# Head 6 aggregated in the block scheme, and the second layer's attention vector products spread over heads 0 to 5

## The chip, the cores and the metric

The kernel runs on one core of a Trainium2 chip. The metric is the device time of one execution in microseconds. TensorE (PE) multiplies matrices, VectorE (DVE) and ScalarE (ACT) do elementwise work, GpSimd (POOL) and SyncE (SP) here mostly issue transfers (DMAs). "PEld" in the profile is TensorE's loading of weights, which overlaps its matmuls.

## The reference, cut to what matters

Two graph attention layers, a residual and a layer norm, for N = 512 nodes and D = 768 features. Layer 1 has H = 8 heads, layer 2 has one.

```python
def gat_layer(x, W, a_s, a_d, b, edge_index, concat):
    h = (x @ W).reshape(n, H, C)
    alpha_s = jnp.einsum('nhc,hc->nh', h, a_s)
    alpha_d = jnp.einsum('nhc,hc->nh', h, a_d)
    e = jax.nn.leaky_relu(alpha_s[src] + alpha_d[dst], NEG_SLOPE)
    # softmax of e over the edges that enter a node -> alpha
    msg = h[src] * alpha[:, :, None]
    out = jax.ops.segment_sum(msg, dst, num_segments=n)
    return out.reshape(n, H * C) + b
h = jax.nn.elu(gat_layer(x, W1, a_src1, a_dst1, b1, ...))   # 512 x 6144
x = layernorm(x + gat_layer(h, W2, a_src2, a_dst2, b2, ...))
```

The kernel treats the graph as a dense 512 x 512 matrix of edge counts, so that a head's attention is a dense matrix P and its aggregation a product with P. The second layer's `h @ W2` is a sum over the heads of layer 1: (head's output, 512 x 768) times (that head's 768 rows of W2).

## The kernel before, in words

There is one instruction stream per engine, written out by hand (no scheduler moves anything); each engine takes its own in that order, and the order in the Python text is therefore the order on each engine. SP's and POOL's transfers too are issued in the order of the text, each once what it overwrites has been read.

First the edge counts are made and heads 0 and 1 are projected (up to L813). Then a loop over h from 0 to 6 (L816) does, for each step:

- **load_w1(h + 2)** (L818): SP loads W1 of the head after next into the tiles of slot "w2" (`w2t1`, `w20`, `w21`), POOL adds a part to them. In the last step the second layer's attention vectors, spread to all 128 rows, go into the tiles `w2t2` and `w2t4` instead, and W2 of head 7 into slot "w2" (L820 to L825).
- **Aggregation of head h**, the product of features and P. In steps 0 to 5 by `mixed` (L741): a block scheme, in which halves of the features times halves of P make seven block products instead of eight. Each of three column groups c runs seven products of two matmuls with 256 columns (L763). It needs sums of blocks, of the features in `gS` (`left_sums`, L717, four VectorE additions of 768 columns) and of P in `pS` (`right_sums`, L730, four of 512 columns). They are made a step earlier, during the projection, and stand between its matmuls. `fill` is a list of VectorE work that `mixed` puts between its own: the attention logits of the next head (`half_logits`, L312). In step 6 by `aggregate` (L705): six column groups c of four matmuls with 512 columns (L709), no sums. Between these VectorE does the next head's logits (c < 2) and then the twelve products of L841: W2 of head 7, row block by row block (k from 0 to 5), times the two attention vectors of layer 2, each summed along the row into `V`. `V` (768 x 2) serves at the end to get head 7's share of the second layer's logits from `gT` directly (L964).
- `elu` (L694) after either kind: ScalarE makes the parts, VectorE joins them into `gT` (L703).
- **load_a(h + 2)** (L845): SP loads the attention vectors `a_s` and `a_d` of the head after next.
- **second** (L347): `gT` times W2 of head h, in a block scheme with matmuls of 384 columns (all by the helper at L304), added up in `h2` and `u2`. Meanwhile VectorE and ScalarE make the attention matrix of head h + 1 (`lift` L448, `leak` L454, `rank` L457, `weigh` L663). In steps 0 to 5 it is transposed by DMA: ScalarE separates the bytes' halves (`turn_out`, L684), SP issues the transpose (L688), ScalarE joins the result into `PT` (`turn_in`, L690). In step 6 TensorE transposes (`turn`, L675) and ScalarE copies (L679). At the end of steps 0 to 5 SP loads W2 of head h + 1.
- **projection** of head h + 2 (steps 0 to 5, L900 to L922): 14 pairs n of a product (L304) and its emptying from PSUM. Right operands that are sums, t2 and t4, lie in `w2t2` and `w2t4`; VectorE makes them with L296 and L297 at n = 1 and 3. P6 (n = 4 and 5) reads t2, P4 (n = 8 and 9) reads t4. L339 empties P6. The sums for the next step's `mixed` stand at n = 1 to 8, but only where the next step uses `mixed`.

After the loop head 7 is aggregated plainly, multiplied by W2, and the second layer's attention, aggregation and layer norm follow.

Of the kernel before, what the change touches and what calls it, by code (L numbers as in the profile page):

```python
# [8 lines left out]
F32 = mybir.dt.float32  # L9
# [27 lines left out]
def gat_pass(  # L37
# [89 lines left out]
    def load_a(h, a_s, a_d):  # L127
        A[h] = []
        for name, a in (("a_s", a_s), ("a_d", a_d)):
            v = wpool.tile([P, D], F32, name=name)  # L130
            nc.sync.dma_start(v, row_bcast(a))
            A[h].append(v)
# [134 lines left out]
    xS = keep.tile([P, 3, HK, HN], F32, name="xS")  # L267
    scr = keep.tile([P, D], BF16, name="scr")
    V = keep.tile([P, DC, 2], F32, name="V")
    al2 = keep.tile([P, 2, NT], F32, name="al2")  # L270
    own2 = keep.tile([P, NT], F32, name="own2")

# [39 lines left out]
    def half_logits(h, t):  # L312
        return [lambda al=al, a=a, sign=sign: nc.vector.scalar_tensor_tensor(
            scr, HS[h][:, t, :], sign, a, op0=ALU.mult, op1=ALU.mult, accum_out=al[:, t:t + 1])
            for al, a, sign in zip(AL[h], A[h], (1.0, -1.0))]

    def logits(h, feats, t):
        for al, a, sign in zip(AL[h], A[h], (1.0, -1.0)):
            nc.vector.scalar_tensor_tensor(scr, feats[:, t, :], sign, a, op0=ALU.mult,
                                           op1=ALU.mult, accum_out=al[:, t:t + 1])  # L320
# [384 lines left out]
    def aggregate(h, c):  # L705

        ps = mm.tile([P, 512], F32, name="mm")
        for s in range(NT):
            nc.tensor.matmul(ps[:, :N], HS[h][:, s, c * P:(c + 1) * P], PT[:, s, :],  # L709
                             start=(s == 0), stop=(s == NT - 1))  # L710
        return elu(h, c, ps[:, :N], slice(0, N), "r")
# [29 lines left out]
    def mixed(h, A_, B_, fill):  # L741

        tt = nc.vector.tensor_tensor
        behind = []

        def some(n):
            for f in fill[:n]:
                f()
            del fill[:n]

        for c in range(HK):
            u = work.tile([P, HN], F32, name="u")
            w = work.tile([P, HN], F32, name="w")
            zr = work.tile([P, N], F32, name="zr", bufs=3)
            bank = {}

            def part(p, over=None):
                if over is None:
                    bank[p] = mm.tile([P, 512], F32, name="mm")
                else:  # L760
                    bank[p] = bank[over]
                for k in range(2):
                    nc.tensor.matmul(bank[p][:, :HN], A_[p][:, k, c * P:(c + 1) * P], B_[p][:, k, :],  # L763
                                     start=over is None and k == 0, stop=k == 1, skip_group_check=True)
                return bank[p][:, :HN]

            nc.scalar.copy(u, part("P1"))  # L767
            if behind:

                behind = behind[0]()  # L770
            tt(u, u, part("P6"), op=ALU.add)
            tt(w, u, part("P7"), op=ALU.add)
            for f in behind[:1]:
                f()
            near_l = elu(h, c, part("P2", over="P1"), near, "l")
            some(1)
            tt(zr[:, far_], part("P5"), w, op=ALU.subtract)
            for f in behind[1:]:
                f()
            tt(zr[:, near], u, part("P4", over="P7"), op=ALU.add)  # L780
            near_l()
            tt(u, part("P3", over="P5"), u, op=ALU.subtract)
            some(-(-len(fill) // (2 * (HK - c) - 1)))

            def others(c=c, u=u, zr=zr):
                return [elu(h, HK + c, zr, slice(0, N), "r", spare=zr), elu(h, c, u, far_, "l", spare=u)]
            behind = [others]
        return behind[0]()
# [24 lines left out]
    for f in rsums[2:]:  # L813
        f()
    besides = [lsums[3], *some_logits]
    for h in range(H - 1):  # L816
        if h + 2 < H:
            load_w1(h + 2)()  # L818
        else:
            A[H] = []  # L820
            for j, a in ((2, a_src2[0]), (4, a_dst2[0])):
                v = wpool.tile([P, HK, HALF], F32, name=f"w2t{j}").rearrange("p k n -> p (k n)")[:, :D]
                nc.sync.dma_start(v, row_bcast(a))
                A[H].append(v)
            last_sum = load_w2(H - 1, "w2")  # L825
        GA, gsums = left(gT, gS)
        if h + 2 < H:
            finish = mixed(h, AA, BB, besides + [p for t in ((0, 1) if h else (0, 1, 3)) for p in half_logits(h + 1, t)])
        else:
            finish = []  # L830
            for c in range(DC):
                finish.append(aggregate(h, c))
                if c:
                    finish.pop(0)()
                if c < 2:
                    logits(h + 1, HS[h + 1], c)
                else:

                    for k in ((0, 1), (2,), (3,), (4, 5))[c - 2]:
                        for v, a, sign in zip(range(2), A[H], (1.0, -1.0)):  # L840
                            nc.vector.scalar_tensor_tensor(scr, W2[H - 1][k // HK][:, k % HK, :], sign, a,  # L841
                                                           op0=ALU.mult, op1=ALU.mult, accum_out=V[:, k, v:v + 1])
        besides = []
        if h + 2 < H:
            load_a(h + 2, a_src1[h + 2], a_dst1[h + 2])  # L845
        pairs = second(h, GA, B2)
        for m, _ in pairs[:2]:
            m()
        pairs[0][1]()
        for f in finish:  # L850
            f()
        gsums[0]()
        pairs[1][1]()
        gsums[1]()
        if pending:
            pending.pop(0)()
        spread(h + 1)
        pairs[2][0]()
        gsums[2]()
        pairs[3][0]()  # L860
        gsums[3]()
        if pending:
            pending.pop(0)()
        pairs[2][1]()
        pairs[3][1]()
        last = h + 2 == H
        q = [lift(h + 1, 0)]
        for n in range(2, 7):
            (m0, e0), (m1, e1) = pairs[2 * n:2 * n + 2]
            m0()  # L870
            if not last:
                m1()
            if n < 6:
                leak(q[n - 2])
                rank(q[n - 2], n - 2)
            if n < 5:
                q.append(lift(h + 1, n - 1))
            if last:

                if n > 3:  # L880
                    turn(q[n - 4], n - 4)
                if n == 6:
                    weigh(q[3], 3)
                m1(lambda: turn(q[3], 3) if n == 6 else None)
            if not last and n == 6:
                turn_in(0)
                weigh(q[2], 2)
                turn_out(q[2], 2)
            e0()
            if last and 2 < n < 6:  # L890
                weigh(q[n - 3], n - 3)
            if not last and 3 < n < 6:
                weigh(q[n - 4], n - 4)
                turn_out(q[n - 4], n - 4)
            if not last and n == 6:
                weigh(q[3], 3)
                turn_out(q[3], 3)
                load_w2(h + 1)()
            e1()
        if h + 2 < H:  # L900
            B_, sums = right(W1[h + 2], "w2")
            pairs = projection(h + 2, XA, B_)
            for n in range(14):
                pairs[n][0]()
                if n == 0:
                    turn_in(1)
                    B2, sums2 = right(W2[h + 1], "w1")
                if n in (1, 3):
                    sums[n // 2]()
                if n == 1:  # L910
                    AA, sums3 = left_sums(h + 1) if h + 3 < H else (None, [])
                pairs[n][1]()
                if n in (2, 4):
                    turn_in(1 + n // 2)
                if n == 5 and h + 3 < H:
                    BB, sums3 = right_sums()
                if 1 <= n < 9 and h + 3 < H:
                    sums3.pop(0)()
                if n in (9, 10):
                    sums2.pop(0)()  # L920
                if n in (11, 13):
                    logits(h + 2, HS[h + 2], 2 + (n - 11) // 2)  # L922
        else:
            last_sum()
            B2, sums2 = right(W2[H - 1], "w1")
# [5 lines left out]
    nc.sync.dma_start(b2_bc, row_bcast(b2))  # L931
    AL[H] = (al2[:, 0, :], al2[:, 1, :])
    GA, gsums = left(gT, gS)
    finish = []
    parts = [(h2[:, 2 + i, L], i, ALU.add) for i in range(2)] + [
        (h2[:, j + i, R], i, ALU.subtract) for j in (2, 0) for i in range(2)]
# [140 lines left out]
```

## Time and profile before

| what | value |
|---|---|
| median of 3 runs (lowest, highest) | 653.67 us (653.57, 653.68) |
| the profiled execution, its span | 653.82 us, 651.8 us |
| TensorE busy | 640.2 us, 98% of the span |
| VectorE busy | 507.4 us, 78% |
| ScalarE busy | 273.8 us, 42% |
| GpSimd busy | 47.0 us, 7% |
| bytes moved by DMA, mean rate | 90.88 MB, 139 GB/s |

How to read it: "busy" sums an engine's instructions over the span; a busy engine need not be the one that sets the end. The chain of work that ended last is followed back from the last instruction to what released it, so it names what did set the end. A group's line gives the number of instructions after "x", then busy time and the mean duration of one in ns; TensorE's matmuls overlap, so that their durations add up to more than their busy time. For each matmul of the text in this data type the trace holds two records. In a timeline, brackets give the idle time ahead of an instruction and what ended it. Some stages by start time: `mixed` of steps 0 to 5 starts at 82.4, 156.5, 229.5, 302.5, 375.7 and 448.7 us, `aggregate` of step 6 at 521.7, of head 7 at 571.6; the final aggregation runs from 623.6 on.

### The profile page before, as it was taken

How to read it: one execution, taken by the hardware profiler on the slowest of the kernel's cores; microseconds unless marked ns; L12 is line 12 of the kernel's file. 1: busy time of each engine (PE TensorE's matmuls, PEld its weight loads, DVE VectorE, ACT ScalarE, POOL GpSimd, SP SyncE). 2: the span in 40 equal slices, each digit the busy share in tenths (PEclk: the TensorE clock that was granted, in tenths of full speed). 3: DMA queues.
4: the chain of work that ended last, by engine and by line, in shares of the span. 5: the costliest groups of instructions: out<-in, count | busy, mean ns of one | idle time of the engine just before them, and what ended most of it. 6: DMA issues, size and time to landing. Idle time of an engine off the chain costs nothing.

```text
span 651.8 us, 7058 instructions
## 1 busy us (share of the span) xinstructions
PE 640.2 (98%) x2347; PEld 397.6 (61%) x2347; DVE 507.4 (78%) x1102; ACT 273.8 (42%) x469; POOL 47.0 (7%) x90
## 2 busy tenths in 40 slices
PE   8999999999999999999999999999999999999995
PEld 4544586557755586557755586557755545645553
DVE  7989989968777777858777777858775588876775
ACT  5774744530736044531736044521736043243440
POOL 1310020011000010011000010011000000000000
PEclk9999999999999999999999999999999999999998
DMA  9993398196506790296406790296407865000122
GB/s 316 328 202 86 74 332 215 37 264 199 123 0 173 157 269 23 45 265 200 112 1 174 169 267 12 49 267 198 108 1 202 203 181 133 24 1 0 34 56 77
DMA packets 74186, 90.88 MB, mean 139 GB/s; under 512 B 36710, under 2 KB 58526, under 8 KB 74142
## 3 DMA queue, kind: packets, MB, share of 16 engines
q1 hardware_dynamic: 60478, 68.72, 33.6%
q0 software_dynamic: 12976, 20.65, 18.3%
q10 hardware_dynamic: 688, 0.98, 0.5%
q8 instruction: 20, 0.33, 0.2%
q14 instruction: 24, 0.20, 0.1%
HBM read 78.02 MB, written 1.57 MB: 122 GB/s over the span
## 4 chain that ended last, share of the span: by engine, by line
PE 97%; ACT 1%; DVE 1%; issue 0%; DVEq 0%
PE mm L304 64%; PE mm L763 17%; PE mm L709 6%; PE mm L1029 3%; PE held L304 2%; PE tr L542 1%; PE bc L177 1%; ACT os L514 1%; PE bc L445 0%; PE bc L542 0%; PE tr L957 0%; PE tr L678 0%; ACT xT L205 0%; PE mm L204 0%; DVE os L516 0%
## 5 line engine op out<-in xcount | busy, mean ns | idle before, releaser
L304 PE MATMUL mm<-w,gT 128*128 128x384 f32 x288 | 97.4, 487 | 0.0
L304 PE MATMUL mm<-w,xT 128*128 128x384 f32 x264 | 88.4, 488 | 0.0
L304 PEld LDWEIGHTS mm<-w,gT 128*128 128x128 f32 x288 | 53.9, 190 | 35.7 <-issue 2.0
L304 PEld LDWEIGHTS mm<-w,xT 128*128 128x128 f32 x264 | 49.8, 190 | 35.7 <-ACT os L514 0.8
L462 ACT ACTIVATE q<-q,nmax 128x512 f32<-128x512 f32 x36 | 25.8, 721 | 89.8 <-DVE nmax L460 89.8
L304 PE MATMUL mm<-w1t,gS 128*128 128x384 f32 x180 | 60.7, 486 | 0.0
L767 ACT COPY u<-mm 128x256 f32<-128x256 f32 x18 | 6.7, 373 | 119.2 <-PE mm L763 119.2
L304 PE MATMUL mm<-w2t,xS 128*128 128x384 f32 x168 | 56.6, 487 | 0.0
L763 PE MATMUL mm<-PT,hs 128*128 128x256 f32 x216 | 52.6, 379 | 0.0
L362 DVE TENSOR_TENSOR h<-h,mm 128x384 f32<-128x384 f32 x72 | 39.6, 551 | 14.4 <-PE mm L304 13.8
L304 PEld LDWEIGHTS mm<-w1t,gS 128*128 128x128 f32 x180 | 34.1, 190 | 23.6
L304 PEld LDWEIGHTS mm<-w2t,xS 128*128 128x128 f32 x168 | 31.8, 190 | 22.4 <-ACT q L451 0.4
L763 PEld LDWEIGHTS mm<-PT,hs 128*128 128x128 f32 x216 | 41.0, 190 | 7.2 <-issue 0.4
L686 ACT COPY nr<-q 128x1024 uint16<-128x1024 uint16 x32 | 33.4, 1044 | 23.2 <-DVE q L672 15.8
L709 PE MATMUL mm<-PT,hs 128*128 128x512 f32 x96 | 41.6, 593 | 0.0
L691 ACT COPY PT<-zr 128x1024 uint16<-128x1024 uint16 x32 | 37.1, 1158 | 2.0 <-DMA zr<-nr 2.0
L763 PE MATMUL mm<-pS,gS 128*128 128x256 f32 x144 | 37.1, 380 | 0.0
L304 PE MATMUL mm<-w,gS 128*128 128x384 f32 x96 | 32.6, 486 | 0.0
L304 PE MATMUL mm<-w1t,gT 128*128 128x384 f32 x96 | 32.5, 487 | 0.0
L304 PE MATMUL mm<-w,xS 128*128 128x384 f32 x96 | 32.5, 487 | 0.0
L709 PEld LDWEIGHTS mm<-PT,hs 128*128 128x128 f32 x96 | 18.2, 190 | 22.9 <-issue 21.5
L106 POOL DMA_DIRECT2D w1t<-in_L_gnn_W_dram x7 | 8.9, 1268 | 312.4 <-PE mm L304 181.3
(184 smaller groups left out, 1068.4 us busy)
## 6 DMA issues: line engine op xcount, KB each, us to landing
w<-in_L_gnn_W_dram SPq DMA_DIRECT2D x90, 384.0 KB, 6.1
w<-in_L_gnn_W_dram POOLq DMA_DIRECT2D x16, 576.0 KB, 9.1
w2t<-in_L_gnn_W_dram SPq DMA_DIRECT2D x10, 576.0 KB, 10.6
w1t<-in_L_gnn_W_dram SPq DMA_DIRECT2D x9, 576.0 KB, 4.6
w2t<-in_L_gnn_W_dram POOLq DMA_DIRECT2D x8, 576.0 KB, 9.6
w1t<-in_L_gnn_W_dram POOLq DMA_DIRECT2D x7, 576.0 KB, 8.5
a_s<-in_L_gnn_a_src_dram SPq DMA_DIRECT2D x8, 384.0 KB, 3.9
a_d<-in_L_gnn_a_dst_dram SPq DMA_DIRECT2D x8, 384.0 KB, 5.4
```

Source lines behind the costliest of these rows:

```text
L106: nc.gpsimd.dma_start(t1, upper[:, :, R], accum_op=ALU.add)
L177: nc.tensor.matmul(idle, zeros[:, :P], zeros, start=True, stop=True)
L304: nc.tensor.matmul(ps[:, :HALF], A_[p][:, k, i * P:(i + 1) * P], B_[p][:, k, :], start=start and k == 0, stop=k == HK - 1, skip_group_chec ...
L362: nc.vector.tensor_tensor(a, a, ps, op=ALU.subtract if p == "P7" else ALU.add)
L462: nc.scalar.activation(q, q, AF.Exp, bias=nmax, scale=-1.0)
L514: nc.scalar.activation(o, nodes, AF.Sign, bias=nidx[:, c:c + 1])
L686: nc.scalar.copy(apart.rearrange("p (h n) -> p h n", h=2), q.bitcast(U16).rearrange("p (n h) -> p h n", h=2))
L691: nc.scalar.copy(PT.rearrange("p s n -> p (s n)").bitcast(U16).rearrange("p (s n h) -> p s n h", s=NT, h=2)[:, :, t * P:(t + 1) * P, :], p ...
L709: nc.tensor.matmul(ps[:, :N], HS[h][:, s, c * P:(c + 1) * P], PT[:, s, :], start=(s == 0), stop=(s == NT - 1))
L763: nc.tensor.matmul(bank[p][:, :HN], A_[p][:, k, c * P:(c + 1) * P], B_[p][:, k, :], start=over is None and k == 0, stop=k == 1, skip_group ...
L767: nc.scalar.copy(u, part("P1"))
L1029: nc.tensor.matmul(ps[:, :cols.stop - cols.start], PT[:, s, t * P:(t + 1) * P], h2[:, s, cols], start=(s == 2), stop=(s == 1))
```

## The change

Head 6 is aggregated by `mixed` too, with the sums for it in the projection of step 5. The products of L841 are gone. In their place `attended(h)`, called after `load_a(h + 2)` in steps 0 to 5, has SP load row block h of head 7's W2 and the layer 2 attention vectors into `w2t2` and `w2t4`, each tile of 1152 columns holding 768 of one thing and 384 of another: four loads per step, in place of none. At n = 0 of the projection, ahead of L296, VectorE does three products with them: 768 columns for the first vector, twice 384 for the second, whose halves go to `V` and to a new tile `V2`. These two are added ahead of head 7.

```diff
@@ -267,6 +267,7 @@
     xS = keep.tile([P, 3, HK, HN], F32, name="xS")
     scr = keep.tile([P, D], BF16, name="scr")
     V = keep.tile([P, DC, 2], F32, name="V")
+    V2 = keep.tile([P, DC], F32, name="V2")
     al2 = keep.tile([P, 2, NT], F32, name="al2")
     own2 = keep.tile([P, NT], F32, name="own2")
 
@@ -813,6 +814,22 @@
     for f in rsums[2:]:
         f()
     besides = [lsums[3], *some_logits]
+
+    def attended(k):
+
+
+        b1_, b2_ = (wpool.tile([P, HK, HALF], F32, name=f"w2t{j}").rearrange("p k n -> p (k n)") for j in (2, 4))
+        nc.sync.dma_start(b1_[:, :D], w2[(H - 1) * D + k * P:(H - 1) * D + (k + 1) * P, :])
+        nc.sync.dma_start(b2_[:, :D], row_bcast(a_src2[0]))
+        for b, cols in ((b2_, L), (b1_, R)):
+            nc.sync.dma_start(b[:, D:], row_bcast(a_dst2[0])[:, cols])
+
+        def times(cols, a, sign, out):
+            return lambda: nc.vector.scalar_tensor_tensor(
+                scr[:, cols], b1_[:, cols], sign, a, op0=ALU.mult, op1=ALU.mult, accum_out=out[:, k:k + 1])
+        return [times(slice(0, D), b2_[:, :D], 1.0, V[:, :, 0]), times(L, b2_[:, D:], -1.0, V[:, :, 1]),
+                times(R, b1_[:, D:], -1.0, V2)]
+
     for h in range(H - 1):
         if h + 2 < H:
             load_w1(h + 2)()
@@ -824,25 +841,11 @@
                 A[H].append(v)
             last_sum = load_w2(H - 1, "w2")
         GA, gsums = left(gT, gS)
-        if h + 2 < H:
-            finish = mixed(h, AA, BB, besides + [p for t in ((0, 1) if h else (0, 1, 3)) for p in half_logits(h + 1, t)])
-        else:
-            finish = []
-            for c in range(DC):
-                finish.append(aggregate(h, c))
-                if c:
-                    finish.pop(0)()
-                if c < 2:
-                    logits(h + 1, HS[h + 1], c)
-                else:
-
-                    for k in ((0, 1), (2,), (3,), (4, 5))[c - 2]:
-                        for v, a, sign in zip(range(2), A[H], (1.0, -1.0)):
-                            nc.vector.scalar_tensor_tensor(scr, W2[H - 1][k // HK][:, k % HK, :], sign, a,
-                                                           op0=ALU.mult, op1=ALU.mult, accum_out=V[:, k, v:v + 1])
+        finish = mixed(h, AA, BB, besides + [p for t in ((0, 1) if h else (0, 1, 3)) for p in half_logits(h + 1, t)])
         besides = []
         if h + 2 < H:
             load_a(h + 2, a_src1[h + 2], a_dst1[h + 2])
+            attend = attended(h)
         pairs = second(h, GA, B2)
         for m, _ in pairs[:2]:
             m()
@@ -904,17 +907,19 @@
                 pairs[n][0]()
                 if n == 0:
                     turn_in(1)
+                    for f in attend:
+                        f()
                     B2, sums2 = right(W2[h + 1], "w1")
                 if n in (1, 3):
                     sums[n // 2]()
                 if n == 1:
-                    AA, sums3 = left_sums(h + 1) if h + 3 < H else (None, [])
+                    AA, sums3 = left_sums(h + 1)
                 pairs[n][1]()
                 if n in (2, 4):
                     turn_in(1 + n // 2)
-                if n == 5 and h + 3 < H:
+                if n == 5:
                     BB, sums3 = right_sums()
-                if 1 <= n < 9 and h + 3 < H:
+                if 1 <= n < 9:
                     sums3.pop(0)()
                 if n in (9, 10):
                     sums2.pop(0)()
@@ -931,6 +936,7 @@
     nc.sync.dma_start(b2_bc, row_bcast(b2))
     AL[H] = (al2[:, 0, :], al2[:, 1, :])
     GA, gsums = left(gT, gS)
+    nc.vector.tensor_tensor(V[:, :, 1], V[:, :, 1], V2, op=ALU.add)
     finish = []
     parts = [(h2[:, 2 + i, L], i, ALU.add) for i in range(2)] + [
         (h2[:, j + i, R], i, ALU.subtract) for j in (2, 0) for i in range(2)]
```

## The prediction

> **What bounds the kernel now.** I read the page first: TensorE is busy 98% of the span, and the chain of work that ended last lies on it almost entirely.
>
> ```profile
> PE 97%; ACT 1%; DVE 1%; issue 0%; DVEq 0%
> ```
>
> So only what shortens TensorE's row of matmuls, or puts a hole into it, moves the time. Next the chain in order of time (start, length, work), where each head's stages stand as merged pieces. From loop step 5 on:
>
> ```profile
> 448.66 18.38 PE mm L763 x84
> 467.04 3.87 PE mm L304 x12
> 470.91 0.44 PE bc L445 x4
> 471.34 50.31 PE mm L304 x156
> 521.66 20.60 PE mm L709 x48
> 542.25 3.87 PE mm L304 x12
> ```
>
> Look at the two ways to aggregate a head. Step 5 uses the block scheme (L763): 42 products, recorded as 84 matmuls, 18.38 us. Step 6 uses the plain one (L709): 24 products, 48 records, 20.60 us. Each piece begins where the one before ends, so TensorE had no hole at either border. Steps 1 to 4 show 18.38 as well; step 0, the first, takes from 82.43 to 101.63, which is 19.20, with two short holes.
>
> Third, the windows by stage (length, busy time and count of each engine, granted clock, DMA share, GB/s):
>
> ```profile
> 448.70:467.00 18.30, 18.30 (x85) 15.80 (x84) 14.59 (x34) 10.81 (x25) 2.53 (x2) 1.00 0.84 230
> 467.00:495.60 28.60, 28.60 (x93) 16.98 (x92) 23.30 (x54) 12.74 (x19) 0.00 (x0) 1.00 0.11 22
> 495.60:521.70 26.10, 26.10 (x82) 15.39 (x81) 11.61 (x18) 5.57 (x8) 2.53 (x2) 1.00 0.87 234
> 521.70:542.25 20.55, 20.55 (x49) 9.09 (x48) 17.79 (x36) 8.92 (x15) 2.53 (x2) 1.00 0.59 155
> ```
>
> The rows are mixed(5), second(5), projection(7) and the plain aggregation of head 6. In none does an engine other than TensorE fill the stage; the clock is 1.00 in all.
>
> **The change part by part.**
>
> *Head 6 in blocks.* Removed: 48 matmul records of 20.60 / 48 = 0.429 us. Added: 84 of 18.38 / 84 = 0.219 us. Gain 20.60 - 18.38 = 2.22 us, all on the path. It has to be judged by these spacings and not by the groups' mean durations (593 ns for 512 columns, 379 for 256): those overlap, and 84 x 0.379 against 48 x 0.593 would call the change a loss of 3.4 us, while the chain shows the gain.
>
> On the cost of many small matmuls the trace has 0.429 us for 512 columns and 0.219 for 256, 2% more per column. The Trainium skill ("TensorE: Matmul & The Clock Gate", section "Back-to-back issue gap") speaks against the change: in a stream of weight loads and matmuls it gives about 81 ns per matmul for 128 columns and 131 for 512, so that narrow ones cost far more per column. A straight line between them, an estimate from that page, makes 98 ns for 256, or 0.746 of the wide one; on the trace's 0.429 that would be 84 x 0.320 = 26.9 us for the block scheme, 6.3 us slower instead of 2.22 faster. The five stages of 18.38 us in this trace decide against it.
>
> *What the block scheme needs around it.* VectorE gets in mixed(6) what it does in mixed(5): 14.59 us in 18.3; the plain stage holds 17.79 in 20.55, of which the attention products of L841 (0.96 each and a read of 0.08) go away. ScalarE goes from 15 to 25 instructions, 8.92 to 10.81 us. Both fit as in steps 1 to 5. The sums of left and right operand for head 6 come into projection(7): four of 0.95 (L724 to L727) and four of 0.68 (L735 to L738), 6.5 us. They stand there in steps 0 to 4 in the same places with TensorE's piece unbroken (50.31 us in four of those steps, 50.46 in one), so I cost them at nothing. projection(7) is the emptiest window for VectorE, 11.61 of 26.10.
>
> At the border to second(6), before the change the products of L841 run over by some 3 us, and the sum L284 begins 4.1 us after TensorE's start there; in step 5 it begins 3.5 us after. The later stage therefore starts no worse. From there on head 6 turns its attention with TensorE's own transposes, paced by matmuls: VectorE waits 0.30 us for TensorE at 562.5 and again at 566.8. That stays.
>
> *Three products per head (steps 0 to 5).* One of 768 columns, 1.00 us from start to next start (L841). The two of 384 columns have no row: lower bound the 256-column form of the same instruction, 0.42; upper bound the 512-column one with its accumulator read, 0.68 + 0.08 = 0.76. I take 0.6, the middle. Sum 1.00 + 2 x 0.6 = 2.2 us, between 1.84 and 2.52. They come at the start of the projection, ahead of L296 on VectorE. Timeline of VectorE in step 4 (start, us, engine, line, ..., idle before it in brackets):
>
> ```profile
> 421.75 0.55 DVE L362 TENSOR_TENSOR h<-h,mm 128x384 f32<-128x384 f32 x1
> 422.21 1.35 DVE L296 TENSOR_TENSOR w2t<-w2t,w 128x1152 f32<-128x1152 f32 x1
> ...
> 425.34 1.35 DVE L297 TENSOR_TENSOR w2t<-w2t,w 128x1152 f32<-128x1152 f32 x1
> 426.61 0.95 DVE L726 TENSOR_TENSOR hs<-hs 128x768 f32<-128x768 f32 x1
> 431.35 0.56 DVE L339 TENSOR_TENSOR hs<-hs,mm 128x384 f32<-128x384 f32 x1 [3.79 <-PE mm L304]
> ```
>
> VectorE sits idle for 3.79 us before L339, because the matmuls it empties aren't done. The 2.2 us go into that hole, and 1.6 are left (1.3 at the upper bound). Steps 0 to 3 have 3.79 to 3.93 there; step 5 will, once it has the sums. What TensorE waits for behind them: L296 (t2) ends at 423.6, then at 425.8, and its first matmul starts at 429.14, a margin of 3.4; L297 (t4) ends at 426.7, then 428.9, and is wanted at 436.88. PSUM banks of the stage before are emptied ahead of the products. So nothing on the path; without the hole it would be up to 2.2 x 6 = 13 us.
>
> *Four loads per head.* 384 + 384 + 192 + 192 = 1152 KB on SP's queue, behind a_d and ahead of the DMA transposes (L688). Their tiles are last read by the projection before, long done. SP's queue and the DMA share of two windows in step 5:
>
> ```profile
> 462.36 0.33 SPq L131 DMA_DIRECT2D a_d<-in_L_gnn_a_dst_dram  x1
> 488.11 9.33 SPq L688 DMA_TRANSPOSE zr<-nr  x4
> ```
> ```profile
> 468.00:472.00 4.00, 4.00 (x17) 2.49 (x16) 2.96 (x6) 2.50 (x6) 0.00 (x0) 1.00 0.00 0
> 472.00:476.00 4.00, 4.00 (x13) 2.30 (x13) 3.77 (x6) 0.07 (x1) 0.00 (x0) 1.00 0.00 0
> ```
>
> Issue costs 4 x 0.33 = 1.3 us of SP, which then waits until 488 anyway. At 230 GB/s the 1.18 MB take 5 us; one behind the other at 10 us each, the slowest landing of a 384 KB row load, they take 40 at the worst and 16 at the usual 3.9. From 463 there are 25 us to the transposes and 32 to the products (495.2); step 0 has 18 us to its transposes. The DMA engines stand at 0.00 there. I take nothing, worst bound in the third rival. POOL's queue gets no instruction; its last sum load no longer waits 13.8 us for L841 and was off the path.
>
> *The addition of V2* (6 columns, some 0.15 us by the one-column L669) stands at the start of head 7, where VectorE idles 2.21 us before and 2.18 after. Nothing.
>
> **Sum.** The profiled execution took 653.82 us: span 651.8 and 2.0 around it. 653.82 - 2.22 = 651.60. It lies 0.15 above the median of the runs shown, 653.67, so the median after is 651.45, 0.34% less.
>
> **The rivals.**
>
> *1. Head 6 runs like step 0.* There the block stage begins before its sums are ready and takes 19.20 us. If in step 5 the sums come late, the gain is 20.60 - 19.20 = 1.40: median 652.27. For: VectorE gets 2.2 us more just there. Against: in step 4 the last sum ends 8.5 us before mixed(5) starts (440.17 against 448.66).
>
> *2. It doesn't do what it says: the time comes back as a wait.* The block stage is 2.22 shorter but second(6) or head 7 waits for VectorE or ScalarE: median 653.67. For: head 7's first matmul already waits 0.03 us for ScalarE's copy at 571.54, so that side has no reserve. Against: that copy follows a transpose and a product which TensorE itself paces, and ScalarE, the busier one in mixed, still idles 1.47 us before its first work of second(5).
>
> *3. The loads land late, slower than before.* The products stand at the head of VectorE's queue and wait for their loads; behind them wait L296 and with it TensorE. It decides if the loads land more than 3.4 us after VectorE gets there, 32 + 3.4 us after their issue; from 3.4 + 2.22 / 6 = 3.8 the change is a loss. At 40 us (four slowest landings in a row) TensorE loses 4.6 us in each of six steps: 27.6 - 2.2 = 25.4, 679.1. One us of loss per step makes 6 - 2.22 = +3.8, 657.5. Against: DMA share 0.00, and loads of this size land in 3.9 us.
>
> **How the numbers follow.** Forecast 0.85, rival 1 0.06, rival 2 0.04, rival 3 0.05. The predicted time is the forecast's, 651.45. The forecast's own band is small: its stages repeat to 0.15 us, runs to 0.1. The range goes from 650.9 to 652.5, so that it takes in rival 1 and leaves out 0.09. A measurement of this kernel can tell about 0.2%, 1.3 us, from no change; rival 1 lies at that border and is halved. Faster 0.85 + 0.03 = 0.88; same 0.03 + 0.04 = 0.07; slower 0.05.
>
> **What would show it.** In the profile after: seven L763 pieces instead of six, the one of head 6 at 18.4 us; L709 with 48 records instead of 96, all in head 7; idle before L339 at about 1.6 us in steps 0 to 5; projection pieces still 50.31; the four loads landed before the transposes. A hole in TensorE's row ahead of the projection's P6 (L296), a head 6 stage over 19 us, or a chain that runs through VectorE or a DMA would prove me wrong.

## The result, and the profile after

| | before | changed |
|---|---|---|
| median | 653.49 us (653.41 to 653.68) | 651.03 us (650.94 to 651.38) |
| ratio | 1 | 0.9962, 95% interval 0.9952 to 0.9972 |
| profiled execution, its span | 653.82, 651.8 us | 651.15, 649.4 us |

The change made the kernel 2.46 us faster (0.38%); the forecast was 2.22 (0.34%). Lines of the changed kernel are counted from here on: L304 has become L305, L296 is L297, L339 is L340, L709 is L710, L763 is L764; the three products are L828.

The chain of the changed kernel in order of time (start, length, work), the pieces around head 6:

```profile
448.27 18.38 PE mm L764 x84
466.65 3.87 PE mm L305 x12
...
470.96 50.31 PE mm L305 x156
521.27 18.38 PE mm L764 x84
539.65 3.87 PE mm L305 x12
```

Head 6's stage is now the same piece as step 5's, 18.38 us where there were 20.60, and the pieces before and behind it join without a hole. Its window and that of the projection ahead of it (length, then busy time and count of TensorE, weight loads, VectorE, ScalarE, GpSimd; clock, DMA share, GB/s):

```profile
521.27:539.65 18.38, 18.38 (x86) 15.87 (x85) 14.60 (x34) 10.84 (x25) 2.53 (x2) 1.00 0.71 185
495.00:521.30 26.30, 26.30 (x83) 15.57 (x82) 19.70 (x31) 5.81 (x8) 2.53 (x2) 1.00 0.87 235
```

TensorE is busy all of both; VectorE went from 11.6 to 19.7 us in the projection and from 17.8 to 14.6 in head 6's stage. What the chain does not say is how near VectorE came to being late. That is read in its own timeline, at the start of the projection of step 4:

```profile
421.82 0.95 DVE L828 SCALAR_TENSOR_TENSOR scr<-w2t,w2t 128x768 bf16<-128x768 f32 x1
...
422.82 0.56 DVE L828 SCALAR_TENSOR_TENSOR scr<-w2t,w2t 128x384 bf16<-128x384 f32 x1
...
423.30 0.55 DVE L828 SCALAR_TENSOR_TENSOR scr<-w2t 128x384 bf16<-128x384 f32 x1
...
423.90 1.36 DVE L297 TENSOR_TENSOR w2t<-w2t,w 128x1152 f32<-128x1152 f32 x1
...
430.96 0.56 DVE L340 TENSOR_TENSOR hs<-hs,mm 128x384 f32<-128x384 f32 x1 [1.71 <-PE mm L305]
```

From the first product to L297 are 423.90 - 421.82 = 2.08 us, and the idle time before L340, 3.79 before, is down by just that, to 1.71. The loads on SP's queue in step 5, and the window rows of 464 to 472 us, where the DMA share was 0.15 and 0.00 before the change:

```profile
461.97 0.33 SPq L131 DMA_DIRECT2D a_d<-in_L_gnn_a_dst_dram  x1
462.35 0.42 SPq L822 DMA_DIRECT2D w2t<-in_L_gnn_W_dram  x1
462.83 0.42 SPq L823 DMA_DIRECT2D w2t<-in_L_gnn_a_src_dram  x1
463.29 1.09 SPq L825 DMA_DIRECT2D w2t<-in_L_gnn_a_dst_dram  x2
487.72 9.35 SPq L689 DMA_TRANSPOSE zr<-nr  x4
```
```profile
464.00:468.00 4.00, 4.00 (x18) 3.13 (x17) 2.44 (x6) 3.71 (x9) 0.00 (x0) 1.00 0.96 324
468.00:472.00 4.00, 4.00 (x16) 2.48 (x15) 3.34 (x6) 2.18 (x5) 0.00 (x0) 1.00 0.06 20
```

Over the six steps they land 4.6 to 8.9 us after their issue; in step 5 the DMA engines are empty again by 472, some 16 us ahead of the transposes.

### The profile page after: what moved, and what is told of

It is laid out like the page before. It is cut to its first block, busy times and chain, and to the rows that moved or that the text cites. A ratio compares the mean times of both kernels' runs of the same rounds, so it can differ in the third digit from the quotient of the medians.

```text
span 649.4 us, 7212 instructions
## 1 busy us (share of the span) xinstructions
PE 637.7 (98%) x2383; PEld 404.2 (62%) x2383; DVE 520.4 (80%) x1141; ACT 276.7 (43%) x481; POOL 47.2 (7%) x90
## 4 chain that ended last, share of the span: by engine, by line
PE 96%; ACT 1%; DMA 1%; DVE 1%; issue 0%; SPq 0%
PE mm L305 64%; PE mm L764 20%; PE mm L710 3%; PE mm L1035 3%; PE held L305 2%; PE tr L543 1%; DMA w<-in_L_gnn_W_dram 1%; ACT os L515 1%; PE bc L446 0%; PE bc L543 0%; PE tr L963 0%; PE tr L679 0%; ACT xT L205 0%; DVE os L517 0%; PE bc L985 0%
## 5 line engine op out<-in xcount | busy, mean ns | idle before, releaser
L305 PE MATMUL mm<-w,gT 128*128 128x384 f32 x288 | 97.4, 487 | 0.0
L305 PE MATMUL mm<-w,xT 128*128 128x384 f32 x264 | 88.4, 488 | 0.0
L305 PEld LDWEIGHTS mm<-w,gT 128*128 128x128 f32 x288 | 53.9, 190 | 35.3 <-issue 1.6
L305 PEld LDWEIGHTS mm<-w,xT 128*128 128x128 f32 x264 | 49.8, 190 | 35.7 <-ACT os L515 0.8
L764 PE MATMUL mm<-PT,hs 128*128 128x256 f32 x252 | 61.3, 379 | 0.0
L305 PE MATMUL mm<-w1t,gS 128*128 128x384 f32 x180 | 60.7, 486 | 0.0
L305 PE MATMUL mm<-w2t,xS 128*128 128x384 f32 x168 | 56.6, 487 | 0.0
L764 PEld LDWEIGHTS mm<-PT,hs 128*128 128x128 f32 x252 | 47.8, 190 | 8.4 <-issue 0.4
L363 DVE TENSOR_TENSOR h<-h,mm 128x384 f32<-128x384 f32 x72 | 39.6, 550 | 14.6 <-PE mm L305 14.0
L305 PEld LDWEIGHTS mm<-w1t,gS 128*128 128x128 f32 x180 | 34.1, 190 | 23.6
L305 PEld LDWEIGHTS mm<-w2t,xS 128*128 128x128 f32 x168 | 31.8, 190 | 22.4 <-ACT q L452 0.4
L764 PE MATMUL mm<-pS,gS 128*128 128x256 f32 x168 | 43.2, 380 | 0.0
L764 PEld LDWEIGHTS mm<-pS,gS 128*128 128x128 f32 x168 | 31.8, 190 | 4.7 <-DVE pS L737 0.4
L305 PE MATMUL mm<-w,gS 128*128 128x384 f32 x96 | 32.6, 486 | 0.0
L305 PE MATMUL mm<-w1t,gT 128*128 128x384 f32 x96 | 32.5, 487 | 0.0
L305 PE MATMUL mm<-w,xS 128*128 128x384 f32 x96 | 32.5, 487 | 0.0
L363 DVE TENSOR_TENSOR u<-u,mm 128x384 f32<-128x384 f32 x28 | 15.4, 552 | 19.0 <-PE mm L305 18.7
```

The source lines that it names most:

```text
L305: nc.tensor.matmul(ps[:, :HALF], A_[p][:, k, i * P:(i + 1) * P], B_[p][:, k, :], start=start and k == 0, stop=k == HK - 1, skip_group_chec ...
L363: nc.vector.tensor_tensor(a, a, ps, op=ALU.subtract if p == "P7" else ALU.add)
```

## The experiments

The theory: the gain is TensorE's time in head 6 alone, and products and loads lie in holes that the trace shows. The rivals: the gain comes from VectorE, which lost twelve products in head 6's stage; or products and loads cost something that hides a larger gain.

**1. Undo the block scheme, keep the products spread.**

```diff
-        finish = mixed(h, AA, BB, besides + [...])
+        if h + 2 < H:
+            finish = mixed(h, AA, BB, besides + [...])
+        else:
+            finish = []
+            for c in range(DC):
+                finish.append(aggregate(h, c))
+                if c:
+                    finish.pop(0)()
+                if c < 2:
+                    logits(h + 1, HS[h + 1], c)
...
-                    AA, sums3 = left_sums(h + 1)
+                    AA, sums3 = left_sums(h + 1) if h + 3 < H else (None, [])
...
-                if n == 5:
+                if n == 5 and h + 3 < H:
...
-                if 1 <= n < 9:
+                if 1 <= n < 9 and h + 3 < H:
```

> The changed kernel with one part undone: head 6 is aggregated plainly again (48 matmul records at the plain line, no sums for it in step 5), while the attention products of layer 2 and their loads stay spread over steps 0 to 5. Theory (the gain is TensorE's time in head 6 alone): the stage is 20.60 us again, 2.2 us more than the changed kernel's 651.03, so 653.2 to 653.4, and the same as before the change within 0.1%. Rival (the gain comes from taking the twelve products off VectorE in head 6): 651.0 to 651.5, VectorE's busy time in the stage some 6 instead of 17.8 us and TensorE no faster for it.

Measured: 653.52 us, ratio to before 0.9997 (0.9988 to 1.0006). All of the gain is gone. The window of head 6's stage in this kernel:

```profile
521.47:542.07 20.60, 20.60 (x50) 9.12 (x49) 9.63 (x18) 8.92 (x15) 2.53 (x2) 1.00 0.63 165
```

VectorE's busy time there fell from 17.8 to 9.6 us, and TensorE's piece is 20.60 as before. (I had written some 6 us; I had forgotten that the logits of two node blocks stay.) Taking work off VectorE gained nothing: it was not what the stage waited for.

**2. Keep the block scheme, leave out products and loads.**

```diff
+    nc.vector.memset(V, 0.0)
+    nc.vector.memset(V2, 0.0)
...
-            attend = attended(h)
...
-                    for f in attend:
-                        f()
```

> The changed kernel without the products of layer 2's attention vectors and without their four loads per step; V and V2 are set to zero once at the start, so head 7's share of the second layer's logits is left out. Theory (products and loads are wholly hidden): 651.0, within 0.1% of the changed kernel, idle before the first emptying of P6 (L340) back at 3.8 us in steps 0 to 5. Rival (they cost something that the gain hides): 650.0 or less, down to 651.03 - 6 x 2.1 = 638.

Measured: 651.16 us, ratio to before 0.9965 (0.9952 to 0.9979), against the changed kernel's 0.9962. VectorE's timeline in step 4:

```profile
426.40 0.95 DVE L729 TENSOR_TENSOR hs<-hs 128x768 f32<-128x768 f32 x1
431.13 0.56 DVE L342 TENSOR_TENSOR hs<-hs,mm 128x384 f32<-128x384 f32 x1 [3.79 <-PE mm L307]
```

The hole is back at 3.79 us and the time has not moved. Eighteen products and 24 loads cost nothing that can be measured.

**3. More products in the same place: where does the cover end?** The three products of each step are done twice, and in a second kernel three times.

```diff
-                    for f in attend:
+                    for f in 2 * attend:      # the second kernel: 3 * attend
```

> The changed kernel with the three products of each step done twice at the same place (2.08 us more of VectorE ahead of L297 in each of six steps). Theory (the hole before L340 is 1.7 us, and TensorE's own margin, from the end of t2 at 425.26 to P6 at 428.76, is 3.5 us): t2 ends at 427.3, TensorE does not wait; 651.0 to 651.1, idle before L340 at 0. Rival (VectorE has no real slack in the projection, any work added there is paid): up to 6 x 2.08 = 12.5 us more, 663.5.

Measured: 651.55 us, ratio to before 0.9964 (0.9951 to 0.9976). That is 0.5 us above the changed kernel's median, where at most 0.1 was expected; the spans do not show it (649.1 to 649.6 us over these executions, 649.2 to 649.5 over the changed kernel's), so it lies outside the span of the instructions.

> The changed kernel with the three products of each step done three times (4.16 us more). Theory (margin 3.5 us in each step): t2 ends at 425.26 + 4.16 = 429.42 where P6 would begin at 428.76; TensorE waits 0.66 us in each of six steps, 651.03 + 4.0 = 655.0 (654.5 to 655.5). If the margin is not what decides: 651.0 (all hidden) or 676 (all paid, 6 x 4.16 = 25).

Measured: 656.02 us, ratio to before 1.0037 (1.0024 to 1.005). VectorE's hole and TensorE's row in step 4, first of the kernel with the products twice, then of the one with the products thrice:

```profile
431.47 0.55 DVE L340 TENSOR_TENSOR hs<-hs,mm 128x384 f32<-128x384 f32 x1
431.93 0.95 DVE L728 TENSOR_TENSOR gS<-hs,gS 128x768 f32<-128x768 f32 x1
433.10 0.55 DVE L340 TENSOR_TENSOR hs<-hs,mm 128x384 f32<-128x384 f32 x1 [0.22 <-PE mm L305]
```
```profile
424.36 7.90 PE L305 MATMUL mm<-w,xT 128*128 128x384 f32 x24
432.82 4.14 PE L305 MATMUL mm<-w2t,xS 128*128 128x384 f32 x12 [0.56 <-DVE w2t L297]
436.80 4.03 PE L305 MATMUL mm<-w,xT 128*128 128x384 f32 x12
```

Twice: the idle time before the first L340 is used up, and the second takes what is left; TensorE's pieces keep their lengths (50.31 us, 18.38). Thrice: P6 finds t2 missing and TensorE waits, for VectorE's L297, as bracketed. So there are two reserves, one behind the other: VectorE's own (1.7 us), and TensorE's margin on t2 (3.5 us). Only the second costs time when it is gone. The size was a little off, and 656.02 lies above the 654.5 to 655.5 that I had given: a step grew from 73.00 to 73.83 us (230.97 to 304.80 between two block stages), 0.83 instead of 0.66. Of this, P6's late start is 432.82 - (424.36 + 7.74) = 0.72, where 7.74 is the time of the 24 records ahead of it. The other 0.11 lies in P6 itself: 436.80 - 432.82 = 3.98 to the next product, and 3.87 where nothing waits. Six times 0.83 are the 5.0 us by which the kernel got slower.

**4. Block scheme in head 6, the twelve products left in its stage.**

```diff
-        finish = mixed(h, AA, BB, besides + [...])
+        if h + 2 == H:
+            besides = besides + [p for t in (0, 1) for p in half_logits(h + 1, t)] + [
+                lambda k=k, v=v, a=a, sign=sign: nc.vector.scalar_tensor_tensor(
+                    scr, W2[H - 1][k // HK][:, k % HK, :], sign, a, op0=ALU.mult, op1=ALU.mult, accum_out=V[:, k, v:v + 1])
+                for k in range(DC) for v, a, sign in zip(range(2), A[H], (1.0, -1.0))]
+            finish = mixed(h, AA, BB, besides)
+        else:
+            finish = mixed(h, AA, BB, besides + [...])
...
-            attend = attended(h)
...
-                    for f in attend:
-                        f()
...
-    nc.vector.tensor_tensor(V[:, :, 1], V[:, :, 1], V2, op=ALU.add)
```

> Head 6 in the block scheme, but the twelve products of layer 2's attention vectors stay in step 6: they come last in the list of VectorE work that the block scheme takes between its own, out of head 7's W2 as before the change; no loads and no products in steps 0 to 5. Theory (the block stage has no room for them: VectorE needs 14.6 + 12 = 26.7 us in a stage of 18.4): VectorE falls behind, gT for the product with W2 comes late, and TensorE waits 4 to 8 us in the stage or just behind it: 655 to 659. That would make the spreading a condition of the gain. Rival (the 2.2 us come from the block scheme wherever the products stand): 651.0 to 651.5.

Measured: 658.71 us, ratio to before 1.0075 (1.0058 to 1.0091): slower than both kernels. TensorE in that stage and behind it:

```profile
533.54 1.13 PE L764 MATMUL mm<-PT,gS 128*128 128x256 f32 x4 [0.69 <-DVE zr L778]
...
539.92 1.13 PE L764 MATMUL mm<-pS,hs 128*128 128x256 f32 x4 [0.94 <-DVE w L773]
541.74 1.13 PE L764 MATMUL mm<-PT,gS 128*128 128x256 f32 x4 [0.69 <-DVE zr L778]
...
549.73 5.54 PE L305 MATMUL mm<-w,gT 128*128 128x384 f32 x12 [2.55 <-DVE u L363]
555.11 4.03 PE L305 MATMUL mm<-w1t,gS 128*128 128x384 f32 x12
```

The same chain that is all TensorE in the changed kernel goes through VectorE here: its instructions between the blocks (L773, L778) come late behind a product, and the last six products hold back the emptying of second's first product (L363). The block stage now takes 21.45 us instead of 18.38, and the wait behind it 2.55. A third part is easily overlooked: the product after that wait takes 555.11 - 549.73 = 5.38 us instead of 3.87, because the granted clock, 1.00 until the wait began, is 0.50 from 549.7 to 551.7 us. The three make 3.07 + 2.55 + 1.51 = 7.1 of the 7.4 us by which the span exceeds the changed kernel's. So taking the products out of head 6's stage gains nothing by itself (experiment 1), but left at this place they cost more than the block scheme gains. No other place for them in step 6 was tried.

**5. The four loads issued late.** They stand behind the load of the next head's W2 instead of behind `load_a`.

```diff
-            attend = attended(h)
...
                 load_w2(h + 1)()
+                attend = attended(h)
```

> The changed kernel with the four loads per step issued later: behind the load of the next head's W2 at the end of the product with W2, instead of behind the attention vectors' loads at its start. Computation unchanged. Theory (VectorE's queue stands still until the loads have landed, and t2 with it): they wait on SP behind seven loads that are issued from 497 to 502, land at about 508 to 512, t2 is ready some 4 us later at 512 to 516 where P6 would begin at 502: TensorE loses 10 to 14 us in each of six steps, 711 to 735. Rival (the loads' place in the queue does not matter since the engines have room): 651 to 655.

Measured: 760.12 us, ratio to before 1.163 (1.160 to 1.166), some 18.2 us per step. VectorE in step 5, then the windows of TensorE's hole and of what follows:

```profile
496.68 0.55 DVE L363 TENSOR_TENSOR h<-h,mm 128x384 f32<-128x384 f32 x1
514.09 0.96 DVE L828 SCALAR_TENSOR_TENSOR scr<-w2t,w2t 128x768 bf16<-128x768 f32 x1 [16.86 <-DMA w2t<-in_L_gnn_a_src_dram]
...
518.07 1.36 DVE L297 TENSOR_TENSOR w2t<-w2t,w 128x1152 f32<-128x1152 f32 x1
```
```profile
504.00:519.40 15.40, 0.24 (x1) 0.00 (x0) 3.44 (x8) 1.53 (x2) 2.53 (x2) 0.66 1.01 281
519.50:523.00 3.50, 3.50 (x6) 2.00 (x7) 3.46 (x4) 0.00 (x0) 0.00 (x0) 0.54 0.00 0
523.00:527.00 4.00, 4.00 (x14) 2.30 (x13) 2.96 (x5) 0.00 (x0) 0.00 (x0) 1.00 0.00 0
```

Here the third rival of the prediction comes true. VectorE stands at its first product for 16.9 us, with the DMA share at 1.01. L297 begins at 518.07 instead of 496.68 + 0.46 + 2.08 = 499.2, so 18.9 late; minus the margin of 3.5 that is 15.4, and TensorE's recorded wait is 15.2. I expected 10 to 14 per step: behind the load of W2 the 192 KB rows take 11.7 us to land (median), 5.4 in the changed kernel. Over the six steps the waits for L297 add up to 94.2 us, 15.7 each. The rest of the 18.2 is a second price: after the hole the granted clock is 0.54 on the mean of 3.5 us, and the piece of 60 matmul records behind it takes 21.2 us in step 5 where an undisturbed one (ahead of step 0) takes 19.55. Step 5 is the mildest of the six; the others take 21.8 to 22.6, and on the mean a step loses 2.5 us to this, which with the 15.7 makes the 18.2. The Trainium skill ("TensorE: Matmul & The Clock Gate", section "What's actually happening") says that TensorE falls to half its clock after an idle window of about 3.4 us. The traces agree on the half, with a clock of 0.50 in the first 3 us behind this hole (step 5), but not on the length: in experiment 4 a wait of 2.55 us was enough, and there the measurement decides. The wait of 0.56 us in experiment 3 left the clock at 1.00.

No experiment points to a version that beats the changed kernel: products and loads have nothing left to give. Head 7 is still aggregated plainly, in 20.87 us; whether the block scheme would pay there was not tried.

## Why the prediction was right, point by point

- **Bound, and the sum.** That TensorE's row sets the end, and that 20.60 gives way to 18.38, is shown by the pieces after and by experiment 1, where putting only this back loses all of the gain. Judging by the spacing of records (0.429 and 0.219 us) and not by their durations was the choice that decided the sign.
- **Size.** 2.46 us measured against 2.22. The median, 651.03, lies 0.42 below the forecast's 651.45: 0.24 of it is this difference, and 0.18 is that the kernel before has 653.49 over six executions, where the forecast started from 653.67 over three. In the two profiles head 6's stage gives 2.22 of it; another 0.35 lies at the start, where the first matmul with weights begins at 7.37 us instead of 7.72. The text of the start is the same in all kernels but for the two settings to zero in experiment 2, and that matmul began at 7.18 to 7.57 us in four of the experiments' profiles, held up by a load in two and by ScalarE in one. So I put the 0.35 down to variation from one execution to the next. No run was made for it, but experiments 1 and 2 bear it out: there it began at 7.55 and 7.51 us, almost alike, and the last VectorE piece of the chain at 646.06 and 643.81, 2.25 apart.
- **Three products.** 2.2 us estimated, 2.08 measured: from start to next start the two of 384 columns take 0.48 and 0.60, where 0.6 was put in for each. Idle before L340 1.71 (1.85 in step 3), 1.6 forecast. Experiments 2 and 3 show the cover and its end.
- **Four loads.** Landed in 4.6 to 8.9 us and hidden, as forecast; experiment 5 gives the price without that cover.
- **Sums in projection(7), border to second(6).** No hole in the pieces: the one of step 5 is 50.31 us with the sums as it was without them. The prediction read the other steps slightly wrong: before the change 50.31 stands in three of steps 0 to 4, 50.46 in step 3 and 50.58 in step 0; nothing hung on it, since after the change they are the same within 0.01. At the border the sum L285 begins 3.5 us after TensorE's start of second(6), as in step 5 before.
- **Rivals.** Rival 1 (19.20) did not come: the stage took 18.38. Rival 2 did not: head 7 begins with the same 0.03 us wait. Rival 3 came only once the loads were issued 40 us later (experiment 5, 503 us against 462).
- **Narrow matmuls.** The prediction's estimate from the two figures of the Trainium skill ("TensorE: Matmul & The Clock Gate", section "Back-to-back issue gap") would have had the stage at 26.9 us; it took 18.38. The measurement decides: 256 columns cost 2% more per column here.

## What to carry to other kernels

Where one engine's row has no holes, count its instructions at their spacing in that row, not at their mean duration. An edit that gains there may need work of other engines to move first; price such work against two reserves in turn, the idle time of its own engine and the margin of the next instruction on the bounding engine, and look where each ends. A load that feeds the head of a busy engine's queue belongs ahead of the large transfers, where the DMA share is low, even tens of us before its use.

## What the runs showed of the hardware that was not expected

A hole cost more than its wait: in experiment 5 TensorE waited 15.7 us per step and came back at a granted clock of 0.54 on the mean of 3.5 us (read in step 5), so that a step lost 18.2 us. In experiment 4 a single wait of 2.55 us was followed by the half clock too, and cost 1.5 us more; one of 0.56 us in experiment 3 was not. And a 192 KB row load that lands in 5.4 us at its place in the changed kernel took 11.7 us behind a W2 load (medians).
